# Attention with 16-wide heads: maxima on the whole array, values' products two tiles at a time

## The chip, the cores and the metric

The kernel runs on one core of a Trainium2 chip. The metric is the device time of one execution in microseconds (us); lower is better. The core has TensorE (PE, with its weight loads shown apart as PEld), VectorE (DVE), ScalarE (ACT), GpSimd (POOL) and SyncE (SP), which here only issues DMAs. Each engine works through its own instructions in a fixed order and waits for the others through semaphores.

## The reference

Two sequences of 512 positions, 512 wide, go through four residual layers: attention a (weights as integer codes, 32 heads of 128), a mixture of low-rank experts, attention b, and the experts again. The change lies in attention b alone, which for a layer-normed x computes:

```python
q = (x @ Wq).reshape(B, T, 32, 16)        # 32 heads of 16, 8 key heads, 4 queries to each
k, v = (x @ Wk), (x @ Wv)                  # 8 heads of 16
q, k = rope(q), rope(k)
att = einsum('bhgqd,bhkd->bhgqk', q, k) / 4
att = where(causal, att, -inf)
ctx = einsum('bhgqk,bhkd->bhgqd', softmax(att), v)
out = ctx.reshape(B, T, 512) @ Wo
```

Everything is in float32. B is 2 and T is 512.

## The kernel before, in words

Attention a and the first experts come first; they take some 807 us and are not touched. Attention b then works on `pairs` (line 700): 32 pairs of key heads (batch b, half kh, query group g, pair pr), each pair with two heads h. A loop (line 931) of 96 + 8 steps gives each pair three steps. Inside it the order on PE is exactly the order in which the code gives its products out (`manual_schedule`, line 932); the other engines' orders are made by the framework's scheduler.

A head's query and key are stored as two rounded parts each (high and low, float32r), spread so that the 64 rows of a product hold 16 dimensions by four combinations of parts. `queries_in` and `keys_in` fetch them by DMA from a scratch tensor in DRAM. Of a pair, head 0 stands in rows 0 to 63 and head 1 in rows 64 to 127 of the tiles `qs` (five in turn, NQ) and `ks` (two). In the half that a head does not use, `ks` holds -1 in two rows and zeros elsewhere, and `qs` later gets the head's maximum in the same two rows, so that one product over 128 rows gives the score less the maximum.

Every pair passes through these parts:

- `maxima` (line 748), three steps: the scores `sc_b` (line 765), for each of the two heads a product over that head's 64 rows, for the query tiles (0, 1), (3,) and (2,). Their widths are 128 and 256, then 512, then 384 columns. DVE adds the causal mask and reduces each to its maximum (`top`, line 769); after the third step POOL splits the maxima into a high and a low part (`mm`, lines 777 and 778).
- `maxima_in` (line 783), two steps later: PE turns mm (`tpm`, line 788), and ACT copies two rows of the result into each head's half of `qs` (line 791).
- `probabilities` (line 796), three steps, eight steps (LEAD) after the maxima: the scores again, turned, over 128 rows (`st_b`, line 812), the exponential on ACT into `pT_b` (line 818), and the causal select on POOL (line 821). Its tiles are (0,), (1,) and (3, 2).
- `weighted_b` (line 831): the values' products `num_b` (line 838). Four heads, that is two pairs, give four products into four groups of 32 columns of the array, for each of the four tiles j, whose widths are 512, 384, 256 and 128. They are collected in `due` and given out one tile at a time, in two of three steps, while more than one (HELD) is waiting.

A step gives out, in this order: queries and the turning of maxima where due, `st_b`, `sc_b`, then `num_b`, and then some of the work beside it (`side`, set by `pace`): the experts of the other batch, projections, and the output product `po`. PE's float32 products appear as two records each, its float32r products (`sc_b`, `st_b`) as one.

The loop's core, before:

```python
            if LEAD <= step:
                next(ps)
            if step < total:
                next(ms)
            col += 2 / 3
            while col >= 1:
                col -= 1
                if len(due) > HELD:
                    due.pop(0)()
```

PSUM tiles of `sc_b`, `st_b` and `tpm` come from one pool of five banks (`ps_x`), `num_b` has one bank of its own, and the exponentials have five tiles of 512 columns and eight of 384.

Of the kernel before, what the change touches and what calls it, by code (L numbers as in the profile page):

```python
# [13 lines left out]
F32R = mybir.dt.float32r  # L14
# [5 lines left out]
P = 128  # L20
# [20 lines left out]
def kernel(  # L41
# [21 lines left out]
    nc = tc.nc  # L63
# [216 lines left out]
    with ExitStack() as actx:  # L280
# [207 lines left out]
        def chain(*stages):  # L488
            for stage in stages:
                yield from stage  # L490
# [11 lines left out]
        for n in range(len(units) + 4):  # L502
            turn = []

            def at(lag):
                if 0 <= n - lag < len(units):
                    g, b, h = units[n - lag]
                    return (g, b, h, f"{g}_{b}_{h}")

            if at(3):  # L510
                g, b, h, nm = at(3)
# [4 lines left out]
            if at(0):  # L516
                g, b, h, nm = at(0)
# [8 lines left out]
            if at(4):  # L526
                g, b, h, nm = at(4)
                turn.append(output(wo[g], h, g * A_G + h, b, *ats.pop((g, b, h)), nm))
            if at(2):
                g, b, h, nm = at(2)  # L530
# [32 lines left out]
    for sp in range(4):  # L563
        for par in range(2):
            at = sp * STRIP + par * B_HD
# [6 lines left out]

    HALF = P // 2
    NQ = 5
    qs = [w2.tile([P, 2, S], F32, tag=f"qs{n}", name=f"qs_{n}") for n in range(NQ)]
    ks = [w2.tile([P, 4, S], F32, tag=f"ks{n}", name=f"ks_{n}") for n in range(2)]

    HM = HALF + 2
    mmp = [w2.tile([P, NT, HM], F32R, tag=f"mm{n}", name=f"mm_{n}") for n in range(2)]

    vpads = [
# [2 lines left out]
    for pad in (*ks, *qs, *vpads, *(mm.bitcast(F32) for mm in mmp)):  # L587
        nc.gpsimd.memset(pad, 0.0)
    for pad in ks:
        for sp in range(4):  # L590
            at = (1 - sp % 2) * HALF
            nc.gpsimd.memset(pad[at : at + 2, sp, :], -1.0)
    for pad in vpads:
        for t in range(NT):
            for kh in range(2):
# [104 lines left out]
    pairs = [  # L700
        (b, kh, g, pr) for b in range(B) for kh in range(2) for g in range(B_G) for pr in range(2)
    ]
    STEPS, LEAD, HELD = 3, 8, 1
    mms, nums, oNs, pTs = {}, {}, {}, {}

    dens = {}
# [13 lines left out]
    kparts, qparts = {}, {}  # L720

    def keys_in(b, kh):

        if kh == 0:
            kparts[b] = spread(khls[b], f"k_{b}", (slice(0, 4, 2), slice(1, 4, 2)))
        for h in range(2):
            nc.sync.dma_start(
                ks[kh][ts(h, HALF), h : 4 : 2, :], kparts[b][:, kh * 4 + h : kh * 4 + 4 : 2, :]
            )

    def queries_halved(p):

# [8 lines left out]

    def queries_in(p):
        _, _, g, pr = pairs[p]
        of = qparts.pop(p)
        for h in range(2):
            nc.sync.dma_start(qs[p % NQ][ts(h, HALF), h, :], of[:, (g % 2) * 4 + pr * 2 + h, :])

    def maxima():

        for p, (b, kh, g, pr) in enumerate(pairs):  # L750
            q, k = qs[p % NQ].bitcast(F32R), ks[kh].bitcast(F32R)
            top = small.tile([P, NT, 2], F32, tag="top", name=f"top_{p}")
            for tiles in ((0, 1), (3,), (2,)):
                sc = [
                    ps_x.tile([P, S], F32, tag="x", name=f"sc_b_{p}_{tiles[0]}_{h}")
                    for h in range(2)
                ]
                parts, at = [], 0
                for i in tiles:
                    n = (i + 1) * P  # L760
                    parts += [(i, n, h, sc[h][:, at : at + n]) for h in range(2)]
                    at += n
                for i, n, h, part in parts:
                    rows = ts(h, HALF)
                    nc.tensor.matmul(  # L765
                        part, q[rows, h, ts(i, P)], k[rows, pr * 2 + h, :n], start=True, stop=True
                    )
                for i, n, h, part in parts:
                    nc.vector.tensor_tensor_reduce(  # L769
                        part, part, tri[:, S - n :], 1.0, -3e38, ALU.add, ALU.max,  # L770
                        top[:, i, h : h + 1],
                    )
                if tiles == (2,):
                    mm = mms[p] = mmp[p % len(mmp)]
                    for h in range(2):
                        at = (1 - h) * HALF
                        nc.gpsimd.tensor_copy(mm[:, :, at], top[:, :, h])
                        nc.gpsimd.tensor_tensor(
                            mm[:, :, at + 1], top[:, :, h], mm[:, :, at].bitcast(F32), ALU.subtract
                        )  # L780
                yield

    def maxima_in(p):

        mm = mms.pop(p).bitcast(F32)
        tp = ps_x.tile([P, S], F32, tag="x", name=f"tpm_{p}")
        for t in range(NT):
            nc.tensor.transpose(tp[:HM, ts(t, P)], mm[:, t, :], ident)
        for h in range(2):
            rows = slice((1 - h) * HALF, (1 - h) * HALF + 2)  # L790
            nc.scalar.copy(qs[p % NQ][rows, h, :].bitcast(F32R), tp[rows, :])


    due = []

    def probabilities():

        for p, (b, kh, g, pr) in enumerate(pairs):
            q, k = qs[p % NQ].bitcast(F32R), ks[kh].bitcast(F32R)
            for tiles in ((0,), (1,), (3, 2)):  # L800
                wide = sum(S - j * P for j in tiles)
                for h in range(2):
                    sp = pr * 2 + h
                    st = ps_x.tile([P, S], F32, tag="x", name=f"st_b_{p}_{tiles[0]}_{h}")
                    pT = ptp.tile(
                        [P, wide], F32, tag=f"pT{wide}", name=f"pT_b_{p}_{tiles[0]}_{h}",
                        bufs=5 if wide == S else 8,
                    )
                    at = 0
                    for j in tiles:  # L810
                        n = S - j * P
                        nc.tensor.matmul(  # L812
                            st[:, at : at + n], k[:, sp, ts(j, P)], q[:, h, j * P :],
                            start=True, stop=True,
                        )
                        pTs[b, kh, g, j, sp] = pT[:, at : at + n]
                        at += n
                    nc.scalar.activation(pT, st[:, :wide], AF.Exp)  # L818

                    diag = pT[:, : len(tiles) * P].rearrange("p (m n) -> p m n", n=P)  # L820
                    nc.gpsimd.affine_select(  # L821
                        diag, diag, [[0, len(tiles)], [1, P]], ALU.is_ge, 0.0,
                        base=0, channel_multiplier=-1,
                    )
                if pr == 1:
                    for j in sorted(tiles):
                        pT4 = [pTs.pop((b, kh, g, j, n)) for n in range(4)]
                        due.append(lambda a=(b, kh, g, j, pT4): weighted_b(*a))
                yield

    def weighted_b(b, kh, g, j, pT):
# [67 lines left out]
    def run(*stages):  # L899
        stages = list(stages)  # L900
        while stages:
            stages = [st for st in stages if next(st, stages) is not stages]
# [24 lines left out]
    half = total // 2  # L927
    banks[:] = BESIDE
    side = chain(later, projections(1))
    pace, left, col = 1.05, 0.0, 0.0  # L930
    for step in range(total + LEAD):
        with tc.manual_schedule(engines={mybir.EngineType.PE}):
            if step == half - 8:
                run(side)
                keys_in(1, 0)
            if step == half - 4:
                side = output_b(0, (0, 1))
                pace, left = 0.38, 0.0
            if step == half + LEAD:
                keys_in(1, 1)  # L940
            if step == half + LEAD + 10:
                side = chain(side, output_b(0, (2, 3)), experts(0, "f2", True))
                pace, left = 1.05, 0.0
            if step == total - 6:
                side = chain(output_b(1, (0, 1)), side)
                pace, left = 1.5, 0.0
            quotients[:] = [q for q in quotients if next(q, None) is not None]
            p, at = divmod(step + 4, STEPS)
            if at == 0 and p % 4 == 3 and p + 1 < len(pairs):
                queries_halved(p + 1)  # L950
            if at == 0 and 2 <= p < len(pairs):
                queries_in(p)
            p, at = divmod(step - 4, STEPS)
            if at == 0 and 0 <= p < len(pairs):
                maxima_in(p)
            if LEAD <= step:
                next(ps)
            if step < total:
                next(ms)

            col += 2 / 3
            while col >= 1:
                col -= 1
                if len(due) > HELD:
                    due.pop(0)()
            left += pace
            while left > 0:
                got = next(side, None)
                if got is None:
                    left = 0.0  # L970
                else:
                    left -= got
    banks[:] = ALONE
    while due:
        due.pop(0)()

    run(*quotients)
    parts(side, 6)
# [92 lines left out]
```

## Time and profile before

| | |
|---|---|
| median of 3 runs | 1130.07 us |
| lowest and highest | 1127.04 and 1130.66 us |
| profiled execution | 1130.42 us |
| its span, first to last instruction | 1128.7 us |
| mean granted PE clock | 0.98 |
| PE, DVE, ACT, POOL busy | 96%, 78%, 54%, 50% of the span |
| maxima's products `sc_b` | 256 matmuls, 807.2 to 1040.3 us |
| scores with the maximum `st_b` | 256 matmuls, 819.5 to 1060.0 us |
| ACT copies of the maximum into qs | 64, 577 ns each |
| DMAs of queries into qs | 64, 128 KB each, 2.8 us to landing |

The profile is of one execution. Matmuls overlap in the array and the end of each is modelled, so the sum of their durations is more than the time they take; the distance between two ends is a better measure. A share of busy time is a mean over stages with different limits. The line of slices cuts the span into 40 parts of 28.2 us; attention b begins at the 29th.

### The profile page before, as it was taken

How to read it: one execution, taken by the hardware profiler on the slowest of the kernel's cores; microseconds unless marked ns; L12 is line 12 of the kernel's file. 1: busy time of each engine (PE TensorE's matmuls, PEld its weight loads, DVE VectorE, ACT ScalarE, POOL GpSimd, SP SyncE). 2: the span in 40 equal slices, each digit the busy share in tenths (PEclk: the TensorE clock that was granted, in tenths of full speed). 3: DMA queues.
4: the chain of work that ended last, by engine and by line, in shares of the span. 5: the costliest groups of instructions: out<-in, count | busy, mean ns of one | idle time of the engine just before them, and what ended most of it. 6: DMA issues, size and time to landing. Idle time of an engine off the chain costs nothing.

```text
span 1128.7 us, 16217 instructions
## 1 busy us (share of the span) xinstructions
PE 1078.9 (96%) x4940; PEld 696.2 (62%) x4940; DVE 878.4 (78%) x2195; ACT 613.2 (54%) x1421; POOL 565.0 (50%) x899
## 2 busy tenths in 40 slices
PE   5799999999999999999999999999899999999988
PEld 3467677677677677677677776555455544444443
DVE  6889899998998998998998889463566667767342
ACT  3556566567566566566566666422175566574410
POOL 2557566566566566566566664262244454333200
PEclk9899999999999999999999999999979989989999
DMA  7301010022011011011021000052422243110000
GB/s 285 112 1 38 1 38 38 1 75 75 1 38 38 1 38 38 1 38 38 1 75 38 1 1 1 1 173 75 157 68 77 56 147 108 34 42 21 20 28 37
DMA packets 24423, 58.11 MB, mean 51 GB/s; under 512 B 3729, under 2 KB 4689, under 8 KB 21777
## 3 DMA queue, kind: packets, MB, share of 16 engines
q1 hardware_dynamic: 24336, 57.08, 15.2%
q8 instruction: 40, 0.66, 0.2%
q14 instruction: 47, 0.38, 0.1%
HBM read 43.30 MB, written 12.58 MB: 50 GB/s over the span
## 4 chain that ended last, share of the span: by engine, by line
PE 81%; DVE 11%; ACT 3%; issue 2%; POOL 2%; DMA 1%; SPq 0%; DVEq 0%; ACTq 0%; POOLq 0%
PE av L429 11%; PE sc L396 10%; PE tp L424 5%; PE py_f L266 5%; PE ps_o L439 5%; PE ps_o L438 5%; PE ph_f L207 5%; PE ps_q L358 5%; PE ps_q L359 4%; PE num_b L838 4%; PE sc_b L765 3%; PE st_b L812 3%; PE po L892 3%; PE pq_b L682 3%; DVE r_q L365 2%
## 5 line engine op out<-in xcount | busy, mean ns | idle before, releaser
L404 ACT ACTIVATE p<-sc,nmx 128x128 f32<-128x128 f32 (+3 forms) x256 | 135.7, 530 | 95.6 <-DVE nmx L399 92.7
L396 PE MATMUL sc<-kT,qT 128*128 128x128 f32 (+3 forms) x512 | 180.2, 433 | 0.7 <-POOL qT L377 0.7
L376 POOL TENSOR_TENSOR r_q<-r_q,tab 128x512 f32<-128x512 f32 x64 | 82.5, 1289 | 190.9 <-DVE rs_q L375 190.9
L365 DVE SCALAR_TENSOR_TENSOR r_q<-ps_q,s_q,r_q 128x512 f32<-128x512 f32 x192 | 143.5, 748 | 37.3 <-PE ps_q L359 23.5
L413 POOL TENSOR_SCALAR p<-p,rden 128x128 f32<-128x128 f32 (+3 forms) x256 | 140.3, 561 | 58.9 <-DVE rden L411 20.6
L425 ACT COPY pT<-tp 128x128 f32<-128x128 f32 (+3 forms) x256 | 109.4, 428 | 104.2 <-PE tp L424 103.6
L769 DVE CUSTOM_DVE_ANT_0 sc_b<-sc_b,tri 128x128 f32<-128x128 f32 (+3 forms) x256 | 119.7, 518 | 58.7 <-PE sc_b L765 53.4
L429 PE MATMUL av<-pT,v 128*128 128x512 f32 (+3 forms) x512 | 148.5, 433 | 0.0
L429 PEld LDWEIGHTS av<-pT,v 128*128 128x128 f32 x512 | 97.0, 190 | 80.2 <-issue 53.9
L448 DVE SCALAR_TENSOR_TENSOR acc<-ps_o,s_o,acc 128x512 f32<-128x512 f32 x186 | 137.5, 739 | 5.5 <-PE ps_o L439 5.4
L399 DVE CUSTOM_DVE_ANT_0 sc<-sc,tri 128x128 f32<-128x128 f32 (+3 forms) x256 | 125.4, 490 | 7.9 <-PE sc L396 7.2
L358 PE MATMUL ps_q<-xh,w_q 128*128 128x512 f32 x256 | 123.8, 484 | 7.6 <-DVE r_q L365 7.6
L818 ACT ACTIVATE pT_b<-st_b 128x384 f32<-128x384 f32 (+1 forms) x192 | 89.8, 518 | 73.5 <-PE num_b L838 50.1
L821 POOL TENSOR_SCALAR_AFFINE_SELECT pT_b<-pT_b 128x128 f32<-128x128 f32 (+1 forms) x192 | 62.5, 333 | 121.1 <-ACT pT_b L818 118.6
L424 PE MATMUL tp<-ident,p 128*128 128x128 f32 x640 | 113.0, 273 | 2.6 <-POOL p L413 2.6
L396 PEld LDWEIGHTS sc<-kT,qT 128*128 128x128 f32 x512 | 96.0, 189 | 24.7 <-ACT p L404 1.3
L438 PE MATMUL ps_o<-ah,w_o 128*128 128x512 f32 x256 | 107.8, 421 | 1.7 <-DVE acc L448 1.0
L439 PE MATMUL ps_o<-al,w_o 128*128 128x512 f32 x256 | 104.9, 410 | 3.5 <-DVE al L152 3.5
L359 PE MATMUL ps_q<-xl,w_q 128*128 128x512 f32 x256 | 102.1, 399 | 0.0
L424 PEld LDWEIGHTS tp<-ident,p 128*128 128x128 f32 x640 | 83.0, 141 | 30.6 <-issue 6.4
L377 POOL TENSOR_TENSOR qT<-r_q,rs_q 128x512 f32<-128x512 f32 x64 | 85.3, 1333 | 1.0
L446 POOL TENSOR_TENSOR acc<-acc,part 128x512 f32<-128x512 f32 x62 | 79.8, 1287 | 10.1 <-ACT part L445 10.1
(181 smaller groups left out, 2027.4 us busy)
## 6 DMA issues: line engine op xcount, KB each, us to landing
codes_q<-in_q_codes_dram SPq DMA_DIRECT2D x8, 1024.0 KB
codes_o<-in_o_codes_dram SPq DMA_DIRECT2D x8, 1024.0 KB, 4.7
spread_q<-hl SPq DMA_DIRECT2D x16, 512.0 KB, 4.4
qs<-spread_q SPq DMA_DIRECT2D x64, 128.0 KB, 2.8
x_a<-in_x_dram SPq DMA_DIRECT2D x8, 256.0 KB, 6.2
codes_k<-in_k_codes_dram SPq DMA_DIRECT2D x2, 1024.0 KB, 6.1
codes_v<-in_v_codes_dram SPq DMA_DIRECT2D x2, 1024.0 KB
x_r<-in_x_dram SPq DMA_DIRECT2D x8, 256.0 KB, 3.6
```

The source lines that it names most:

```text
L358: nc.tensor.matmul(ps, w[:, c, ts(h, A_HD)], xh[b][:, c, :], start=True, stop=False)
L359: nc.tensor.matmul(ps, w[:, c, ts(h, A_HD)], xl[b][:, c, :], start=False, stop=True)
L365: nc.vector.scalar_tensor_tensor(r, ps, s, r, ALU.mult, ALU.add)
L396: nc.tensor.matmul(sc[:, :n], qT[:, ts(i, P)], kT[:, :n], start=True, stop=True)
L399: nc.vector.tensor_tensor_reduce(sc[:, :n], sc[:, :n], tri[:, S - n :], -(A_HD**-0.5), 3e38, ALU.add, ALU.min, nmx,)
L404: nc.scalar.activation(pr, sc[:, :n], AF.Exp, bias=nmx, scale=-1.0, accum_out=den[:, i % 2 : i % 2 + 1],)
L413: nc.gpsimd.tensor_scalar(prs[j], prs[j], rden[:, j % 2 : j % 2 + 1], 1.0, ALU.mult, ALU.mult)
L424: nc.tensor.transpose(tp[:, j, :], prs[i][:, ts(j, P)], ident)
L429: nc.tensor.matmul(av[:, j * P :], v[:, j, :], pT[:, j, j * P :], start=(j == 0), stop=(j == NT - 1))
L438: nc.tensor.matmul(ps, w[:, h, ts(n, P)], ah, start=True, stop=False)
L439: nc.tensor.matmul(ps, w[:, h, ts(n, P)], al, start=False, stop=True)
L448: nc.vector.scalar_tensor_tensor(to, ps, s, to, ALU.mult, ALU.add)
```

## The change

Maxima: both heads of a pair now stand in rows 0 to 63, and rows 64 and 65 take the maximum for both. `sc_b` runs over all 128 rows, one head at a time. Because rows 64 and 65 of a `qs` tile still hold the maxima of the pair that used it five pairs ago, and `ks` holds -1 there, they are cleared on POOL after each fetch of queries from the sixth pair on (27 clearings). Queries and keys come in one DMA instead of two. The tile `mm` keeps its two column places, so `tpm` is the same, and ACT copies both heads' rows to rows 64 and 65.

Values: each tile in `due` carries the step from which it may be given out. When the second one in line is due, two are given out together: tiles 0 and 1 in one step, 2 and 3 in the next.

```diff
-    HALF = P // 2
+    HALF, HM = P // 2, P // 2 + 2
...
     for pad in ks:
-        for sp in range(4):
-            at = (1 - sp % 2) * HALF
-            nc.gpsimd.memset(pad[at : at + 2, sp, :], -1.0)
+        nc.gpsimd.memset(pad[HALF:HM], -1.0)
...
-        for h in range(2):
-            nc.sync.dma_start(
-                ks[kh][ts(h, HALF), h : 4 : 2, :], kparts[b][:, kh * 4 + h : kh * 4 + 4 : 2, :]
-            )
+        nc.sync.dma_start(ks[kh][:HALF], kparts[b][:, ts(kh, 4), :])
...
-        of = qparts.pop(p)
-        for h in range(2):
-            nc.sync.dma_start(qs[p % NQ][ts(h, HALF), h, :], of[:, (g % 2) * 4 + pr * 2 + h, :])
+        q = qs[p % NQ]
+        nc.sync.dma_start(q[:HALF], qparts.pop(p)[:, ts((g % 2) * 2 + pr, 2), :])
+        if p >= NQ:
+            nc.gpsimd.memset(q[HALF:HM], 0.0)
...
-                    rows = ts(h, HALF)
                     nc.tensor.matmul(
-                        part, q[rows, h, ts(i, P)], k[rows, pr * 2 + h, :n], start=True, stop=True
+                        part, q[:, h, ts(i, P)], k[:, pr * 2 + h, :n], start=True, stop=True
                     )
...
-            rows = slice((1 - h) * HALF, (1 - h) * HALF + 2)
-            nc.scalar.copy(qs[p % NQ][rows, h, :].bitcast(F32R), tp[rows, :])
+            at = (1 - h) * HALF
+            nc.scalar.copy(qs[p % NQ][HALF:HM, h, :].bitcast(F32R), tp[at : at + 2, :])
...
-                        due.append(lambda a=(b, kh, g, j, pT4): weighted_b(*a))
+                        due.append((p * STEPS + LEAD + 2 * (j > 0) + (j > 1), (b, kh, g, j, pT4)))
...
-            col += 2 / 3
-            while col >= 1:
-                col -= 1
-                if len(due) > HELD:
-                    due.pop(0)()
+            if len(due) > 1 and due[1][0] <= step:
+                for _ in range(2):
+                    weighted_b(*due.pop(0)[1])
...
     while due:
-        due.pop(0)()
+        weighted_b(*due.pop(0)[1])
```

More of the change, by code (lines that the diff above doesn't have):

```diff
@@ L579 @@
     ks = [w2.tile([P, 4, S], F32, tag=f"ks{n}", name=f"ks_{n}") for n in range(2)]
-    HM = HALF + 2
     mmp = [w2.tile([P, NT, HM], F32R, tag=f"mm{n}", name=f"mm_{n}") for n in range(2)]
@@ L702 @@
     ]
-    STEPS, LEAD, HELD = 3, 8, 1
+    STEPS, LEAD = 3, 8
     mms, nums, oNs, pTs = {}, {}, {}, {}
@@ L929 @@
     side = chain(later, projections(1))
-    pace, left, col = 1.05, 0.0, 0.0
+    pace, left = 1.05, 0.0
     for step in range(total + LEAD):
```

## Prediction

> **What bounds the kernel now.** I read the page's busy shares and slices first, then the chain that ended last, then the busy time by stretch, then the order in time inside the stage that is changed. TensorE (PE) is busy for 96% of the span and makes 81% of the last chain. The changed stage (attention b, first maxima product 807.2 us, last values' product 1063.8) is the right third of the slices.
>
> ```profile
> PE 1078.9 (96%) x4940; PEld 696.2 (62%) x4940; DVE 878.4 (78%) x2195; ACT 613.2 (54%) x1421; POOL 565.0 (50%) x899
> ...
> PE   5799999999999999999999999999899999999988
> ...
> PEclk9899999999999999999999999999979989989999
> ...
> PE 81%; DVE 11%; ACT 3%; issue 2%; POOL 2%; DMA 1%; SPq 0%; DVEq 0%; ACTq 0%; POOLq 0%
> ...
> 830.00:880.00 50.00, 50.00 (x303) 28.14 (x301) 30.51 (x128) 30.13 (x71) 22.03 (x72) 0.97 0.24 77
> 880.00:930.00 50.00, 47.80 (x264) 23.74 (x262) 34.07 (x118) 30.05 (x63) 23.77 (x69) 0.90 0.35 112
> 930.00:980.00 50.00, 47.15 (x274) 23.02 (x274) 37.14 (x130) 29.22 (x61) 21.51 (x77) 0.97 0.27 78
> ```
>
> In the last three rows (stretch, length, then busy PE, PEld, DVE, ACT, POOL, then clock) PE is full or nearly so and the others stand at 43 to 74%. So PE's own order sets the pace here, with some stalls, and the question is what PE does with the time. The timeline of PE shows it (start, duration, what; several equal instructions in a row are one line):
>
> ```profile
> 880.20 0.49 PE L765 MATMUL sc_b<-ks,qs 64*128 64x512 f32 x2
> 880.62 1.06 PE L838 MATMUL num_b<-pT_b,vpad 128*32 128x512 f32 x8
> 881.62 1.98 PE L682 MATMUL pq_b<-wq,xnT_b 128*128 128x512 f32 x4
> 883.04 1.03 PE L812 MATMUL st_b<-qs,ks 128*128 128x512 f32 x2
> 884.00 0.45 PE L765 MATMUL sc_b<-ks,qs 64*128 64x384 f32 x2
> 884.37 0.66 PE L675 MATMUL tpq<-ident,rot_qb 128*128 128x128 f32 x4
> 884.78 0.59 PE L812 MATMUL st_b<-qs,ks 128*128 128x384 f32 x2
> ```
>
> Read the ends (start plus duration) and subtract neighbours; that is what each group occupies. Two full-array products st_b of 512 columns: 884.07 - 883.60 = 0.47, 0.235 each. Two of 384: 885.37 - 885.03 = 0.34, 0.17 each. The maxima's pair of 384 (sc_b, 64 rows each, two heads in the two halves of the array) runs side by side, yet takes 884.45 - 884.07 = 0.38, as much as two full-array ones one after the other: 0.175 for both, and about 0.20 for changing into the split form. The four pq_b records take 883.60 - 881.68 = 1.92, where four times 0.429 is 1.72: again 0.20, for changing back from num_b, the values' products in four 32-column groups. num_b itself: 881.68 - 880.69 = 0.99, twice 0.429 and 0.13 for the change from rows to columns. Over all changes of form in the stage whose neighbours did not wait, the medians are 0.195 into rows, 0.197 back to the full array, 0.118 into columns.
>
> **The change part by part.**
> (1) Changes of form. In the built order there are now 95 into rows, 40 from rows to full, 55 from rows to columns, 7 from full to columns, 61 from columns to full: 95 x 0.195 + 40 x 0.197 + 62 x 0.118 + 61 x 0.197 = 45.7 us. With maxima on all 128 rows and two tiles' values together, 33 into columns and 33 back remain: 33 x (0.118 + 0.197) = 10.4. Gain 35.3 us.
>
> (2) The heads no longer run side by side. sc_b then has the form of st_b (128*128, same types), which is the nearest row. Pair of 512: one more 0.235, less the 0.003 between the pair's ends, 0.232. Pair of 384: 0.172. Group 128, 128, 256, 256: undisturbed now 0.233 without the change of form (0.061 and 0.172); st_b's group of the same four widths takes 0.46, held by weight loads of which each now counts, so +0.229. Together 0.633 x 32 pairs of heads = 20.3 us. Net on PE: -15.0 us.
>
> Here a rule speaks against the change. The Trainium skill, TensorEngine Tiling (Array Packing), Theoretical Speedup, promises up to twice the speed where the contracted dimension is 64 or less. By it alone the change only loses: 1130.4 + 20.3 = 1150.7. The rows confirm the side by side (ends 0.003 apart) but charge about 0.4 us for going in and out, at 0.235, 0.175 and 0.23 us of content. The same page (Key Properties) says that changing the tiling mode drains the engine, without a figure; the trace has the figure, so I take the rows.
>
> (3) POOL's clearing: 27 memsets of 2x1024. The nearest rows are the memset of 128x1024, 950 ns, and that of 2x512, 561: 0.95 us each, 25.6 us of POOL.
>
> ```profile
> L588 POOL MEMSET qs<- 128x1024 f32 x5 | 4.5, 950 | 0.0
> L592 POOL MEMSET ks<- 2x512 f32 x8 | 4.5, 561 | 0.3
> ```
>
> POOL is 43 to 48% busy here, and 0.95 us per three steps of about 2.4 us adds 13%. In POOL's order the memset stands after the selects of the second tile and before the two of tiles (3, 2) of the pair five earlier, which wait for ACT's exponentials (0.48 each) of the same products that the memset waits for. About half lies in that wait; the selects come up to 0.5 us later. Their readers, the values' products, come a step later behind st_b, sc_b and the first batch. The maximum's copies (mm) of another pair stand behind them by a step's maxima on DVE. I take 0; bounds 0 and 25.6. The maxima's own wait for it is covered: it is given out four steps ahead. Set-up memsets of ks: eight of 0.56 against two of at most 1.81, -0.9 to +0, under PE's work.
>
> (4) DMAs: 32 fewer query issues and 4 fewer for keys, of some 0.54 us each on SP, the same bytes, now into 64 partitions. A landing takes 2.8 us and is asked for four steps ahead, nearly 10 us; even twice as long is hidden. SP's order around the spread and denominator DMAs keeps its shape. 0.
>
> (5) Waits. PE already stalls; the view of waits gives what ends them:
>
> ```profile
> ACT pT_b L818 <- PE num_b L838: 50.1, 29, 4.3
> ...
> PEld sc_b L765 <- DVE top L769: 11.8, 30, 0.8
> ...
> PEld tpm L788 <- POOL mm L778: 9.0, 13, 2.2
> ...
> PEld st_b L812 <- ACT pT_b L818: 6.7, 17, 1.0
> ```
>
> The tightest chain is the maximum's: the last sc_b pair (384), DVE's reduction, POOL's mm, PE's transposes tpm. From that pair's end to mm's end it takes 1.75 us (median of 32; 1.5 to 3.2). PE's work in between, summed from the order with the spacings above, is 2.74 us in the median before and 2.53 after, but in a quarter of the pairs under 1.8, because value groups that used to lie in between are moved to two neighbouring steps in six. With the same latencies the uncovered rest sums to 5.7 us before and 8.7 after: +3. Uneven steps (a first batch of 512 and 384 columns takes 0.86 + 0.64 + 0.32 = 1.8 us at one place, with DVE and ACT waiting behind it) cost something more: +1, a guess bounded by 0 and 4. Against it, ACT's exponentials now wait 50 us for num_b to free their buffers, since the last tiles are held until the next group starts; after, all four tiles are gone two steps after they come. That can return 0 to 4 us of PE's waits for ACT; I take 0.
>
> Half clock: in two stretches the granted clock is 0.50 though PE shows as busy.
>
> ```profile
> 819.70:833.30 13.60, 12.96 (x43) 6.75 (x42) 9.70 (x39) 10.18 (x19) 6.17 (x19) 0.50 0.14 46
> ...
> 908.40:918.70 10.30, 10.05 (x34) 4.67 (x38) 5.09 (x21) 4.42 (x10) 4.01 (x12) 0.50 0.54 187
> ```
>
> Both follow stalls. At most half of these 23.9 us, 12, could return; the first lies in the stage's start, where no other work covers, and stays. I take 0 and keep -8 to +6.
>
> Sum: -35.3 + 20.3 + 3 + 1 = -11.0 on the profiled 1130.42 us (span 1128.7 and 1.7 around it), which stands 0.35 above the median of the runs, 1130.07. That gives **1119 us**. The end stays as it is: the last denominators are covered by nine py_f products of 0.86 (eight and four transposes now) against a chain of 8.1 us.
>
> **The rivals.**
> (A) The gain is swallowed: the steps are held by the maximum's chain and by DVE (74% busy in 930 to 980), so that only the full stretches (830 to 895, and about as much again later) give their share, half of 15, less 4 for stalls: 1127 us. For it: the waits above. Against: PE is without a gap for 50 us at a time.
> (B) More than forecast: released buffers and fewer half-clock stretches return 4 and 6 us besides: 1109.
> (C) Slower: the clearing comes onto the path. Place: POOL's queue before the mm copies and the late selects; price up to 0.95 us per pair. It decides from 15.0 / 27 = 0.56 us exposed each; wholly exposed it is 1130.4 - 15.0 + 25.6 = 1141. For it: POOL works strictly in order, and mm already ends PE's waits. Against: the memset is free to start a whole step before mm's maxima are there.
> (D) It does not do what it says: the full-height sc_b keeps a change of form. st_b next to pq_b or tpm shows none (0.23 and 0.06, plain streaming), so this is next to excluded.
>
> **How the numbers follow.** Forecast 0.60 (1113 to 1124), A 0.20, B 0.10, C 0.09, D 0.01. About 0.3% (3.4 us) is what a measurement of this kernel can tell from no change. A lies by a third within that and a small part of it beyond on the slow side; C is wholly slower: faster 0.81, same 0.07, slower 0.12. The range leaves out the outer part of B, and C but for its mild end: 1109 to 1130.
>
> **What would show it.** In the new profile: sc_b as 128*128; a pair of 384 after st_b taking 0.35 and the next group no 0.20; pq_b after sc_b at 0.429 per record; num_b in lines of x16. tpm's waits for mm some 3 us longer, ACT's wait for num_b far under 50. POOL's memsets of 0.95 with the mm copies still waiting for DVE. It is wrong if sc_b's 512 pair takes clearly more than 0.47, if tpm or st_b wait over 15 us longer than before, or if clocks of 0.50 spread.

## The result and the profile after

The changed kernel takes 1118.40 us in the median of 4 runs (1116.07 to 1119.21), the kernel before 1130.37 beside it; the ratio is 0.9895, with a 95% interval of 0.9869 to 0.9921. The profiled execution took 1118.06 us, 12.4 less than the one of before; its span is 1116.3 us. Of the page after, the rows that answer to those shown of before:

```profile
PE 1060.7 (95%) x4940; PEld 708.8 (63%) x4940; DVE 880.8 (79%) x2195; ACT 617.4 (55%) x1421; POOL 587.4 (53%) x920
...
PE   5799999999999999999999999999989989999988
...
PEclk9999999999999999999999999999989999999999
...
PE 80%; DVE 10%; ACT 3%; POOL 3%; issue 2%; DMA 1%; SPq 0%; ACTq 0%; DVEq 0%; POOLq 0%
```

PE is still the engine on the last chain. What changed in its order stands in the timeline of PE (start, duration, what):

```profile
882.53 1.03 PE L805 MATMUL st_b<-qs,ks 128*128 128x512 f32 x2
883.40 0.52 PE L758 MATMUL sc_b<-ks,qs 128*128 128x384 f32 x2
883.84 0.86 PE L831 MATMUL num_b<-pT_b,vpad 128*32 128x256 f32 x16
884.63 0.66 PE L671 MATMUL tpq<-ident,rot_qb 128*128 128x128 f32 x4
885.04 0.60 PE L805 MATMUL st_b<-qs,ks 128*128 128x384 f32 x2
885.48 0.62 PE L758 MATMUL sc_b<-ks,qs 128*128 128x128 f32 x4
...
889.74 0.62 PE L758 MATMUL sc_b<-ks,qs 128*128 128x384 f32 x2
890.20 1.88 PE L678 MATMUL pq_b<-wq,xnT_b 128*128 128x512 f32 x4
```

By the ends again: the pair of 384 takes 883.92 - 883.56 = 0.36, which is two full-array products and nothing for a change of form. The group of 128, 128, 256 and 256 takes 886.10 - 885.64 = 0.46. The four pq_b records after a pair of 384 take 892.08 - 890.36 = 1.72, four times 0.43, without the 0.197 that a full-array product paid behind a split one. num_b comes in lines of 16 records, two tiles at once. All of these are the values that the sum used.

The waits went another way than the streaming. Rows of the view of waits of the kernel after (who waited for whom: us in total, times, longest):

```profile
PEld tpm L781 <- POOL mm L771: 14.3, 16, 2.1
...
PEld st_b L805 <- ACT pT_b L811: 7.2, 23, 0.7
PE tpm L781 <- POOL mm L771: 7.0, 8, 1.9
...
PEld sc_b L758 <- DVE top L762: 4.2, 14, 0.9
```

The two waits of tpm for mm make 21.3 us, where the kernel before had 9.0 (shown above) and

```profile
PE tpm L788 <- POOL mm L778: 3.5, 4, 2.0
```

They are not of one kind. Weight loads (PEld, busy for 63% of the span) run beside the products (PE, busy for 95%), so a weight load's wait is in part covered by products that still run. The rows of PE itself are time in which no product ran, and there the wait for mm rose from 3.5 to 7.0. The wait of sc_b for top fell from 11.8 to 4.2, and ACT's 50.1 us of waiting for num_b with its exponentials is gone. By stretch, the clock is the new thing (stretch, length, busy PE, PEld, DVE, ACT, POOL, clock, DMA share, GB/s):

```profile
821.80:832.00 10.20, 9.23 (x30) 6.99 (x30) 7.89 (x29) 9.00 (x16) 5.52 (x16) 0.50 0.10 27
...
880.00:930.00 50.00, 45.94 (x302) 27.21 (x295) 36.80 (x132) 33.24 (x69) 31.70 (x85) 1.00 0.37 108
930.00:980.00 50.00, 45.56 (x277) 26.51 (x277) 39.63 (x138) 31.47 (x63) 26.66 (x80) 1.00 0.32 89
```

From 880 to 980 PE now has 46 of 50 us busy where it had over 47, at the full clock, where before the means were 0.90 and 0.97. One stretch at half clock is left in the stage, 10.2 us at its start, out of 34.1 us in four (the prediction lists the two longest). The products themselves are slower there: the eight records of num_b with 512 columns took 1.93 us at half clock in the kernel before, against 1.06 at 880.62 in its timeline above.

```profile
911.22 1.93 PE L838 MATMUL num_b<-pT_b,vpad 128*32 128x512 f32 x8
```

### The profile page after: what moved, and what is told of

Same layout as the page of the kernel before. It is cut to its first block, busy times and chain, and to the rows that moved or that the text cites. A ratio compares the mean times of both kernels' runs of the same rounds, so it can differ in the third digit from the quotient of the medians.

```text
span 1116.3 us, 16200 instructions
## 1 busy us (share of the span) xinstructions
PE 1060.7 (95%) x4940; PEld 708.8 (63%) x4940; DVE 880.8 (79%) x2195; ACT 617.4 (55%) x1421; POOL 587.4 (53%) x920
## 4 chain that ended last, share of the span: by engine, by line
PE 80%; DVE 10%; ACT 3%; POOL 3%; issue 2%; DMA 1%; SPq 0%; ACTq 0%; DVEq 0%; POOLq 0%
PE av L429 11%; PE sc L396 11%; PE tp L424 5%; PE ps_o L439 5%; PE ps_o L438 5%; PE ps_q L358 5%; PE ph_f L207 5%; PE ps_q L359 5%; PE num_b L831 3%; PE st_b L805 3%; PE py_f L266 3%; PE sc_b L758 3%; PE pq_b L678 2%; PE po L885 2%; DVE r_q L365 2%
## 5 line engine op out<-in xcount | busy, mean ns | idle before, releaser
L396 PEld LDWEIGHTS sc<-kT,qT 128*128 128x128 f32 x512 | 95.6, 189 | 25.3 <-ACT p L404 2.0
L446 POOL TENSOR_TENSOR acc<-acc,part 128x512 f32<-128x512 f32 x62 | 79.9, 1288 | 10.2 <-ACT part L445 10.1
```

Source lines behind the costliest of these rows:

```text
L396: nc.tensor.matmul(sc[:, :n], qT[:, ts(i, P)], kT[:, :n], start=True, stop=True)
```

## The experiments

The theory under test: the gain is the changes of form that PE no longer makes, less what the heads gained by running side by side. The rivals: the gain comes from buffers freed sooner (ACT's wait for num_b), or part of it is lost to POOL's clearing or to the maximum's chain. The ratios are to the kernel before in runs on the same chip, with 95% intervals; the kernel before had 1126.5 to 1127.4 us there, and the changed kernel, measured twice more, 0.9906 (0.9892 to 0.9920; 1115.69 us) and 0.9896 (0.9879 to 0.9913; 1115.54 us). Both kernels are thus some 3 us faster there than in the first runs (1130.37 and 1118.40), from which the expectations start, so an expectation is judged by its distance from the kernel that it starts from.

**Values alone.** The kernel before with only the giving out of the values' products changed:

```diff
-            col += 2 / 3
-            while col >= 1:
-                col -= 1
-                if len(due) > HELD:
-                    due.pop(0)()
+            if len(due) > 1 and due[1][0] <= step:
+                for _ in range(2):
+                    weighted_b(*due.pop(0)[1])
```

> The kernel before with the values' products alone changed: two tiles together, maxima still side by side on 64 rows. Theory (changes of form): 95 into rows, 33 rows to columns, about 62 rows to full and 33 columns to full, 18.5 + 3.9 + 12.2 + 6.5 = 41.1 us against 45.7 before, so -4.6 us, less about 1 for uneven steps: 1126 to 1127 us. Rival (buffers): the gain comes from num_b freeing the exponentials' tiles sooner; then this kernel shows most of the whole gain, 1119 to 1122, and ACT's wait for num_b falls from 50 us to near nothing with it.

Measured: 1126.68 us, ratio 0.9998 (0.9988 to 1.0009): no change. Both were too hopeful; 1126 to 1127 meant 3 to 4 us less than the kernel before. ACT's wait of pT_b for num_b is no longer among its waits, so the buffers are free sooner, and the time does not move: as the source of the gain, the rival is out. But the 4.6 us that PE saves are not there either. Its waits of tpm for mm went from 12.5 to 18.0 us, on PE itself from 3.5 to 6.1:

```profile
PEld tpm L788 <- POOL mm L778: 11.9, 13, 2.2
...
PE tpm L788 <- POOL mm L778: 6.1, 7, 2.0
```

**Maxima alone.** The changed kernel with the old way of giving out:

```diff
-            if len(due) > 1 and due[1][0] <= step:
-                for _ in range(2):
-                    weighted_b(*due.pop(0)[1])
+            col += 2 / 3
+            while col >= 1:
+                col -= 1
+                if len(due) > HELD:
+                    due.pop(0)()
```

> The changed kernel with the values' products given out as before, one tile at a time. Theory (changes of form): no split rows left, 62 changes into columns and 62 back, 19.5 us against 45.7; less 20.3 for heads one after the other: -5.9 us on PE, with 0 to 3 us of it lost to the maximum's chain: 1124 to 1127. So the two halves should make about 10.5 of the 15.0 us, and 4.5 belong to both together, since a value group after full-array products pays the way in and the way back where after split rows it paid the smaller way in. Rival (buffers): nearly nothing or slower, 1129 to 1134, as PE's streaming grows by 20.3 us and ACT still waits about 50 us for num_b.

Measured: 1122.14 us, ratio 0.9955 (0.9940 to 0.9971), 5.1 us faster, where the term was -5.9 with 0 to 3 lost. ACT still waits 45.7 us for num_b. So the wider maxima gain without the buffers, and pairing the values' tiles gains another 0.5 to 0.6% only on top of them: alone it did nothing.

**Half rows.** The changed kernel, one head at a time, with the split form back and nothing else:

```diff
-    part, q[:, h, ts(i, P)], k[:, pr * 2 + h, :n], start=True, stop=True
+    part, q[:HALF, h, ts(i, P)], k[:HALF, pr * 2 + h, :n], start=True, stop=True
```

> The changed kernel with one edit: the maxima's products name rows 0 to 63 only, still one head at a time, with the clearing kept. The same columns stream, in the same order; only the form of sc_b is split again, without anything side by side. Theory (changes of form): 96 into rows at 0.195, about 63 back at 0.197 and 33 from rows to columns in place of full to columns: 18.7 + 12.4 = 31 us of PE come back, of which stalls take up a part: 1140 to 1149 us, with sc_b after st_b at the ends' distance of 0.37 (384) and the group after it 0.2 late. If changes of form are not the cause: within 3 us of the changed kernel, 1115 to 1122.

Measured: 1147.57 us, ratio 1.0179 (1.0161 to 1.0197), 30.8 to 32.0 us above the changed kernel (0.9906 and 0.9896). Same columns, same order, only the rows named differ. Its timeline of PE:

```profile
884.93 0.71 PE L805 MATMUL st_b<-qs,ks 128*128 128x512 f32 x2
885.57 0.62 PE L758 MATMUL sc_b<-ks,qs 64*128 64x384 f32 x2
886.12 1.12 PE L678 MATMUL pq_b<-wq,xnT_b 128*128 128x512 f32 x2
```

The pair of 384 takes 886.19 - 885.64 = 0.55, that is 0.35 and 0.20, and the two pq_b 887.24 - 886.19 = 1.05, that is 0.86 and 0.19. So naming half of the rows costs 31 to 32 us in all, and the changes of form are in the timeline at their counted price. That the total is also the counted 31 us, with nothing taken up by stalls, is in part chance: tpm's two waits for mm fell from 21.3 to 13.0 us, while the time at half clock in the stage rose from 10.2 to 47.8.

This kernel also prices the other term: it differs from the one with the values alone by running the heads one after the other (and by the layout of rows and the clearing), and stands 1.0179 - 0.9998 = 1.81% above it, 20.4 us, good to some 2 us by the two intervals. The prediction had 20.3. Here too the time at half clock differs (24.1 us in the kernel with the values alone), so the agreement is closer than this run can show.

**Clearing twice.**

```diff
         if p >= NQ:
             nc.gpsimd.memset(q[HALF:HM], 0.0)
+            nc.gpsimd.memset(q[HALF:HM], 0.0)
```

> The changed kernel with POOL's clearing of rows 64 and 65 given out twice, 27 more memsets of about 0.95 us, 25.6 us more of POOL. My step (cost 0): within 2 us of the changed kernel, 1116 to 1121. Rival (the clearing lies on the path ahead of the select and the maximum's copies): each memset exposed in part, +6 to +20 us, 1124 to 1138, with PE's waits for mm and ACT's for num_b longer by as much.

Measured: 1122.78 us, ratio 0.9968 (0.9956 to 0.9980), 7 to 8 us above the changed kernel. The wait of tpm for mm rose from 21.3 to 31.0 us:

```profile
PEld tpm L782 <- POOL mm L772: 19.3, 17, 2.1
...
PE tpm L782 <- POOL mm L772: 11.7, 10, 1.9
```

If a second clearing costs that much, the first may not be free either. Two kernels test it.

**Clearing by a DMA.**

```diff
-            nc.gpsimd.memset(q[HALF:HM], 0.0)
+            nc.sync.dma_start(q[HALF:HM], ks[1 - pairs[p][1]][HM : HM + 2, :2, :])
```

> The changed kernel with rows 64 and 65 cleared by a DMA on SP's queue from rows of the other key tile that are always zero, in place of POOL's memset. Since the second clearing added some 10 us to PE's waits for mm, I now hold that the first costs something as well. Theory (clearing on the maximum's chain through POOL): 3 to 7 us less than the changed kernel, PE's waits for mm down from 21 to 12 to 16 us. Rival (the first memset lies in POOL's idle time, only a second one spills over): within 1.5 us of it. If SP's 27 more issues of 0.54 us get in the way of the query fetches, slower, with waits of sc_b for a DMA.

Measured: 1119.80 us, ratio 0.9939 (0.9925 to 0.9952), 0.3% slower than the memset; the wait for mm is 19.4 us. Neither of the first two readings holds: POOL is 25 us emptier, and the kernel is some 4 us slower. The third, SP's issues in the way of the fetches, has the right sign, but the view of waits shows no wait of sc_b for a DMA, so the cause of the loss stays open.

**No clearing.** The memset left out, and

```diff
-        nc.gpsimd.memset(pad[HALF:HM], -1.0)
+        nc.gpsimd.memset(pad[HALF:HM], -1e-4)
```

> The changed kernel without the clearing: left out are the 27 memsets of rows 64 and 65, and the keys' rows there hold -0.0001 in place of -1, so that the maximum is in effect not subtracted and the stale rows do no harm. All other instructions and waits stay. It prices the first clearing, since the DMA in its place brought waits of its own. If it is free: within 1.5 us of the changed kernel beside it. If it costs as much as the second one did (about 7 us): 5 to 9 us less, PE's waits for mm at 12 to 16 us in place of 21.

Measured: 1116.38 us, ratio 0.9903 (0.9887 to 0.9918), against 1115.54 beside it. The wait for mm is 14.8 + 7.7 = 22.5 us, as with the clearing. The first clearing is free, within the 2 us or so that these runs can tell. The timeline of POOL in the changed kernel shows why:

```profile
888.18 0.95 POOL L740 MEMSET qs<- 2x1024 f32 x1 [0.78 <-PE st_b L805]
889.44 1.16 POOL L814 TENSOR_SCALAR_AFFINE_SELECT pT_b<-pT_b 128x256 f32<-128x256 f32 x3 [0.31 <-ACT pT_b L811]
```

POOL idles 0.78 us until PE's st_b lets the memset go (square brackets: idle before, and what ended it), and after it another 0.31 us until ACT's exponential lets the select go. POOL waited for st_b like this ahead of 26 of the 27 memsets, 25.3 us in all. Without the memset it would idle until the exponential all the same; a second memset of 0.95 us does not fit into the 0.31 us that are left.

**Turning the maxima a step later.**

```diff
-            p, at = divmod(step - 4, STEPS)
+            p, at = divmod(step - 5, STEPS)
             if at == 0 and 0 <= p < len(pairs):
                 maxima_in(p)
```

> The changed kernel with the turning of the maxima (tpm) given out one step later, five steps after the pair's first maxima instead of four; nothing is added or taken away on any engine. Theory (what PE saves is partly given back waiting for the maximum's chain): the 21 us of PE's waits for mm fall to under 5, and the time by 4 to 12 us, less where st_b then waits for ACT's copy. Rival (PE would wait elsewhere instead, DVE and ACT set the pace once PE is faster): within 2 us, with the waits moved to top and pT_b.

Measured: 1116.02 us, ratio 0.9909 (0.9893 to 0.9925): no change, though tpm's waits for mm are nearly gone. The rival holds as to the time. Of the waits, sc_b's for pT_b rose from 3.4 to 10.8 us and st_b's for qs from 3.6 to 5.9; those for top, which it named too, did not rise much:

```profile
PEld sc_b L758 <- ACT pT_b L811: 10.8, 24, 1.1
...
PEld st_b L805 <- ACT qs L784: 5.9, 11, 0.8
...
PEld tpm L781 <- POOL mm L771: 1.8, 2, 0.9
```

**Four tiles together.**

```diff
-            if len(due) > 1 and due[1][0] <= step:
-                for _ in range(2):
+            if len(due) > 3 and due[3][0] <= step:
+                for _ in range(4):
```

> The changed kernel with all four tiles of a value group given out together, in the step of its last tile: 16 changes into columns and back instead of 33, 17 x 0.315 = 5.4 us less. Theory (changes of form alone): -5.4 us, 1113 where the changed kernel has 1118. Rival (uneven steps): 2.4 us of values' products in one place make the other engines run dry and put ACT's exponential behind num_b for its fifth tile of 512; then the same or slower, 0 to +6 us, with ACT's wait for num_b back at 10 us or more. The kernel with the values alone changed, which gained nothing where 3.6 us were expected, speaks for the rival.

Measured: 1116.05 us, ratio 0.9906 (0.9892 to 0.9921): no change. ACT waits 10.0 us for num_b again, as the rival said, and the 5.4 us of PE are gone elsewhere.

**Turning later for pairs 6 to 13 alone**, and the same **with four tiles** (this diff and the last):

```diff
-            p, at = divmod(step - 4, STEPS)
-            if at == 0 and 0 <= p < len(pairs):
-                maxima_in(p)
+            for lag in (4, 5):
+                p, at = divmod(step - lag, STEPS)
+                if at == 0 and 0 <= p < len(pairs) and lag == (5 if 6 <= p < 14 else 4):
+                    maxima_in(p)
```

> The changed kernel with the turning of the maxima one step later for the pairs 6 to 13 alone, where the side work fills PE. Turning all later gained 0.7 and 1.4 us in the cycles of pairs 8 and 10 and lost 0.8, 1.7 and 0.9 in those of pairs 4, 14 and 20. If the two effects are of the place: 1.5 to 2.5 us less than the changed kernel. If they cancel through the queue behind (what is gained comes back as a wait in the next stretch): within 1 us.

> The last one and all four tiles of a value group together. Each alone moved little; if the four tiles' 5.4 us were hidden by the waits for mm that the later turning removes, both together give 3 to 6 us less than the changed kernel; if DVE's and ACT's queues set the pace of these stretches, no more than 2.

Measured: 0.9900 (0.9882 to 0.9918; 1115.97 us) and 0.9904 (0.9887 to 0.9920; 1116.41 us), the changed kernel 0.9896 beside them. From one maxima product of 512 columns to that two pairs on (starts in the timeline), the changed kernel needs 15.39 and 16.25 us at pairs 8 and 10 and the kernel with the later turning 14.68 and 14.84, 2.1 us less; at pairs 14 and 16 it is 12.69 and 12.02 against 14.45 and 13.00, 2.7 us more. What one stretch gains, the next gives back. No version beat the changed kernel.

**The changed kernel again**, the reference of these runs:

> The changed kernel once more, as the reference on the chip of the runs beside it. Ratio to the kernel before as measured first, 0.987 to 0.992, if the gain does not depend on the chip.

> The changed kernel, as the reference on the chip beside the three others: ratio to the kernel before 0.988 to 0.992.

Both as expected.

## Why the prediction was right

The forecast was 1119 us, the runs gave 1118.4. The mechanism is the one that was named: products in a split form cost more for going in and out than side by side saves. That the number came within 1 us is in part luck: the clock, put at 0, returned an estimated 4 to 5 us, and losses that were not counted took about as much.

(1) and (2), the changes of form and the heads one after the other. The distances between ends after are those that were put in. The runs bear out their size, each together with what it moves in waits and clock: 31 to 32 us for the split form where the counts make 31 (expectation of the half rows), 20.4 against 20.3 for side by side. Side by side works as the Trainium skill, TensorEngine Tiling (Array Packing), Theoretical Speedup, says (two ends 0.003 us apart), and loses because each visit is too short for its way in and out.

(3) The clearing: 27 memsets of 946 ns, at no cost that could be measured, shown by the kernel without it. Of the two reasons given, the timeline bears out that POOL waits there anyway. The other, that the maximum's copies stand far enough behind, holds for one memset and no longer for two.

(4) The DMAs: no wait for the query fetches among the longer waits of PE. Not tried alone.

(5) The waits, put at +4 together. PE's idle time shows them directly: of the 249 us from 807 to 1056, PE ran no product for 9.8 us before and 15.1 after, 5.3 more (first and last row of the last section). The part for the maximum's chain, put at +3, is +3.5 in PE's own rows (3.5 to 7.0); the chain's latency, taken as it was, grew from 1.75 to 1.88 us in the median. The wait of sc_b's weight loads for top, not counted, fell by 7.6.

Half clock, put at 0 with bounds of -8 to +6, is the term that was mis-sized. The prediction saw two of the four stretches, 23.9 of 34.1 us, and let none return; 24 us of the 34.1 are gone, which is worth at most half, 12 us. The last section estimates 4 to 5 us. With -15 on PE, +5 of waits and -4 to -5 of clock the sum would be -14 to -15, while the runs gave -10.6 to -12.0. So 2 to 4 us of loss are not accounted for (waits of weight loads that show as busy PE are a candidate, not tested), and they happen to offset the clock.

Where the rest went: the later turning and the four tiles show that taking away PE's longest wait or more of PE's work moves nothing now; the waits turn up at ACT's pT_b and qs instead. That is rival A at work on part of the gain, not on the whole of it. DVE has 40 of 50 us busy from 930 to 980, ACT 31. Which of these queues sets the pace there was not settled. Rivals C and D fell by the runs without clearing and with half rows. Of B's two returns, the freed buffers alone gave nothing; the clock's came, at the estimated 4 to 5 us where B had 6, and the losses hid it.

The end: nine py_f products cover the last chain, as forecast. The stage itself, first maxima product to last values' product, went from 256.6 to 246.0 us in the profiled executions, although it now holds some 3 us more of the experts' products; what follows it went from 64.9 to 61.0. It starts 2.2 us later, ahead of anything changed; a stretch of 3.4 us of half clock at 753 us can explain at most 1.7 of that. Over all the profiled executions here this start lies anywhere from 806.8 to 810.2.

## What to carry to other kernels

Read what a small product costs from the end before it to the end of the next full one, not from its own duration: two side by side can be dearer than one after the other when each visit to a split form holds only 0.2 us of work. Keep short products in the form of their neighbours, and gather those that need another form. And price a part of a change alone as well as together: here one half gained only once the other was there, and once PE's order had been shortened, further savings on PE came back as waits.

## What the runs showed of the hardware

Changing the array's form cost 0.195 to 0.20 us into and out of products of 64 rows, with or without anything running side by side; it cost 0.118 into groups of 32 columns and 0.197 out of them. Not expected: the split-row kernels ran longer at half clock. Over 807 to 1056 us, in this order the kernel before, values alone, half rows, maxima alone and the changed kernel (the last of the three times):

```profile
807.00:1056.00 249.00, 239.18 (x1326) 122.54 (x1325) 167.93 (x623) 146.45 (x305) 100.34 (x332) 0.93 0.25 75
```

```profile
807.00:1056.00 249.00, 236.17 (x1344) 125.38 (x1344) 167.62 (x624) 147.58 (x307) 98.60 (x330) 0.95 0.26 75
```

```profile
807.00:1056.00 249.00, 239.75 (x1222) 129.46 (x1220) 163.32 (x601) 138.35 (x280) 117.08 (x334) 0.90 0.26 76
```

```profile
807.00:1056.00 249.00, 238.21 (x1396) 139.23 (x1396) 170.14 (x625) 155.62 (x315) 129.07 (x367) 0.98 0.25 74
```

```profile
807.00:1056.00 249.00, 233.87 (x1405) 142.88 (x1405) 170.25 (x627) 155.80 (x315) 126.66 (x367) 0.98 0.25 75
```

The mean clock in the stage is 0.90 to 0.95 with split rows and 0.98 without. PE shows as busy for 236 to 240 us in the former and 234 to 238 in the latter, so its busy time does not tell the two apart. These rows are single executions, but the clock of every execution is on record and says the same. Over the whole span it was 0.980 to 0.986 in 45 executions of the kernel before and 13 of the values alone, 0.975 to 0.981 in 5 of the half rows, 0.986 to 0.990 in 6 of the maxima alone, and 0.989 to 0.994 in 14 of the changed kernel.

How much time that is worth can be estimated from the same record. Among executions of one and the same kernel, 0.001 more clock goes with 0.5 us less time (a slope over 123 executions; 0.6 us for the 45 of the kernel before alone). The changed kernel's clock is 0.008 above that of the kernel before beside it, which makes 4 to 5 us of its gain of 11 to 12; the half rows' clock is 0.013 below the changed kernel's, 6 to 8 of their 31 to 32 us. These are estimates: a stall may lower the clock and lengthen the run as well, and what lowers the clock was not tried. That naming 64 rows costs the time is shown; how it divides between the changes of form themselves and the clock that comes with them is open.
